# Cross-attention on one core: the first 512 keys of the probabilities stay unscaled, and their factors are applied when the values' product is copied out

## The chip, the cores and the metric

The kernel runs on one core of one Trainium2 chip. The metric is the device time of one execution in microseconds, the lower the better. Three runs of the kernel before took 2043.12, 2043.25 and 2043.85 us; the median is 2043.25 us. All data are float32. The core's engines are named as in the profile: PE (TensorE, the matmuls), PEld (its weight loads), DVE (VectorE), ACT (ScalarE), POOL (GpSimd) and SP (SyncE, which issues most DMAs).

## The reference, cut to what matters

Two cross-attention layers follow each other, over 8 batches with 100 queries, 20 heads of 32 columns, and a context of 722 tokens: 77 "text" tokens and 645 "ip" tokens. Each head has two softmaxes, one over the text keys and one over the ip keys, and their two products with the values are added:

```python
def attend(q, k, v):                       # one head: (S, 32), (L, 32), (L, 32)
    return softmax(q @ k.T / sqrt(32)) @ v
# layer 0
hs = attend(q, k_text, v_text) + attend(q, k_ip, v_ip)
x = hs @ Wo.T + bo + x
# layer 1: the ip scores get a term per (query, key), the ip probabilities a mask per query
hs = attend(q, k_text, v_text) + (softmax(q @ k_ip.T / sqrt(32) + 0.5 * sem) * mask[:, None]) @ v_ip
out = hs @ Wout + bout + x
```

Here q, k and v are projections of x and of the context; `sem` comes from a small attention of its own. The projections of the context (8 x 645 tokens x 1024, into 640 columns of keys and of values, for each of the two layers) are most of the arithmetic.

## The kernel before, in words

**Two streams of work.** The kernel forms the keys and values of a pair of batches ("production", tiles `psk_*`, `psv_*`, `psvk_*` with a Strassen-like scheme of seven products) and writes them to DRAM, and meanwhile it runs the attention of batches whose keys and values were made earlier. The order of PE, DVE and ACT is written out by hand (`manual_schedule` with the list `PINNED`, line 44): the loop at the end of the kernel goes through `ORDER`, 80 *steps* `(u, c)`, where `u` is one of 16 (layer, batch) units and `c` one of 5 groups of four heads. Between the pieces of a step it places production tasks by a plan of times (`production`, `between`). POOL and SP keep the order in which the instructions are recorded, or what the scheduler makes of it; POOL has little besides the DMAs that write the products to DRAM (lines 652, 691, 694, 811, 814, 841, 914).

**One step.** Steps are counted here from 0 to 79. In step n, with `last` for step n-1, the recorded order is: `scores(n, 0)` against the first 512 keys; production; `transposes(last, 0)` and `(last, 1)`; production; `transposes(last, 2)` and `(last, 3)`; `scores(n, 1)` against the other 210 keys (133 ip, 77 text); production; `transposes(last, 4)` and `(last, 5)`; production; `values(last)`. From step 74 on (`few`) the third stretch of production comes behind `transposes(last, 5)`. Where this text says t0 to t5 it means these six groups of four transposes (line 1099), one per block of 128 keys.

**The softmax of a step** (`scores`). The four heads' scores fall in two PSUM tiles. DVE takes the maxima (line 1003 in layer 0; line 1009 in layer 1, where it also adds `sem` and writes the sum to `p`). ACT takes the exponentials (line 1017) into the tile `p` of 100 queries x 4 heads x 722 keys, with the row sums. The two ranges of the ip keys have maxima of their own, so each has a correction factor `f`. `factors` (lines 1039 to 1043, DVE) combines the sums into `mul`, two factors per query and head (first 512 keys; the other 133), and `rz`, the text's reciprocal sum. Then `p` is scaled in place: ACT multiplies the first 512 keys of each head (`scaled`, line 1049, four instructions a step), DVE the 133 (line 1057) and the 77 (line 1053).

**Who runs what, when.** Exponentials, factors and scalings are not recorded in place but put on the list `later`, and `emit` hands them out between production tasks. `transposes(u, c, 0)` begins with `emit(len(later))`: whatever of the running step is then on the list (the exponentials of its first 512 keys) goes into ACT's queue ahead of the copies of t0.

**Transposes and values.** PE transposes `p` block by block into PSUM, 4 heads x 100 queries wide; the 400 columns are copied to the tile `pt`, by DVE for t0, t1, t3, t5 (line 1106) and by ACT for t2 and t4 (line 1104; in the transposes after the last step t0 too). `values` multiplies `pt` with the values (line 1122, 24 matmuls of 100 columns, four heads side by side in 32 columns of the array each) and DVE copies the 128 x 100 result into `hs` (line 1126), from which `out_piece` (line 904) makes the layer's output; for the last pair `last_out` does it (line 956, `pso_last`), in pieces between the last steps and behind them.

**Buffers.** `ps_pt` has two PSUM buffers, taken in turn by t0 to t5, by `values`, and by the small products (`pso`, `psq`, `psm`); so t2 must wait until t0 is copied out, and t3 until t1 is. `hs` has one buffer in the pool `one`, for a group of two units; a new group's first write must wait until `out_piece` has read the old one. `stats` holds maxima, sums and factors of a step.

Of the kernel before, what the change touches and what calls it, by code (L numbers as in the profile page):

```python
# [9 lines left out]
F32 = mybir.dt.float32  # L10
AF = mybir.ActivationFunctionType
ALU = mybir.AluOpType
AX = mybir.AxisListType

P = 128
B = 8
S = 100
# [3 lines left out]
NI = 645  # L21
NL = NI - 5 * P
NK = NI + NT
KA = 512
KB = NK - KA
H = 20
D = C // H
NC_ = C // P
# [10 lines left out]
PAIRS = [(2 * i, 2 * i + 1) for i in range(NU // 2)]  # L39

ORDER = [(u, c) for u in range(NU - 2) for c in range(NC_)]
# [5 lines left out]
def two_layer_xattn(  # L47
# [17 lines left out]
    nc = tc.nc  # L65
# [21 lines left out]
    ident = const.tile([P, P], F32, tag="ident", name="ident")  # L87
# [17 lines left out]
    wide = {}  # L105
# [152 lines left out]
    with ExitStack() as es:  # L258
# [6 lines left out]
        for k in range(NC_):  # L265
            t = fp.tile([P, C], F32, tag="wr", name=f"wq0_{k}", bufs=NCC)
            rows = wq[0][k * P : (k + 1) * P, :]
# [26 lines left out]
        ps = product_ps("zeros_ps")  # L294
# [4 lines left out]
        for g in range(B // 2):  # L299
            t = fp.tile([P, 2, NC_, S], F32, tag="q", name=f"q0_{g}", bufs=2)  # L300
            ps = [product_ps(f"psq_{g}_{i}") for i in range(3)]
            for k in range(NC_):
                for c in range(NC_):
                    at = c % 2 * 2 * S
                    nc.tensor.matmul(  # L305
                        ps[c // 2][:, at : at + 2 * S], lhsT=wq0[k][:, c * P : (c + 1) * P],
                        rhs=xt[:, 2 * g : 2 * g + 2, k, :],
                        start=(k == 0 and c % 2 == 0), stop=(k == NC_ - 1), skip_group_check=True,
# [174 lines left out]
    stat = ctx.enter_context(tc.tile_pool(name="stat", bufs=3))  # L483
# [483 lines left out]
            nc.sync.dma_start(out[LAST[i] % B][:, c0:c1], resg[g][:, i, c0:c1])  # L967


    pr, stats, sct = {}, {}, {}  # L970

    later = []

# [8 lines left out]
    def scores(u, c, part):  # L982
        k0, k1 = ((0, KA), (KA, NK))[part]
        if part == 0:
            pr[u, c] = ppool.tile([S, 4, NK], F32, tag="p", name=f"p_{u}_{c}")

            stats[u, c] = stat.tile([S, 14, 4], F32, tag="st", name=f"st_{u}_{c}")
        else:
            free_scores()

        scs = [ps_sc.tile([P, 2, 512], F32, tag=f"sc{h}", name=f"sc_{u}_{c}_{part}_{h}") for h in range(2)]
        for i in range(4):
            rows = slice(32 * i, 32 * i + 32)
            nc.tensor.matmul(  # L994
                scs[i // 2][:S, i % 2, : k1 - k0], lhsT=qs_[u][rows, c, :], rhs=ks[u, c][rows, k0:k1], start=True, stop=True
            )
        p, st, l = pr[u, c], stats[u, c], u // B
        n = min(k1, NI) - k0
        lo, f, rz, mul = st[:, 6, :], st[:, 7:9, :], st[:, 9:11, :], st[:, 11:13, :]

        def maxima(h):
            if l == 0:
                nc.vector.tensor_reduce(  # L1003
                    st[:, part, 2 * h : 2 * h + 2], scs[h][:S, :, :n], AX.X, ALU.max, negate=True
                )
                return
            for i in (2 * h, 2 * h + 1):

                nc.vector.tensor_tensor_reduce(  # L1009
                    out=p[:, i, k0 : k0 + n], in0=scs[h][:S, i % 2, :n], in1=sems[u][:, k0 : k0 + n], scale=-1.0,  # L1010
                    scalar=3.0e38, op0=ALU.add, op1=ALU.min, accum_out=st[:, part, i : i + 1],
                )

        def exponentials(h):
            for i in (2 * h, 2 * h + 1):
                dst = p[:, i, k0 : k0 + n]
                nc.scalar.activation(  # L1017
                    dst, dst if l else scs[h][:S, i % 2, :n], AF.Exp, bias=st[:, part, i : i + 1],
                    scale=-1.0 if l else 1.0, accum_out=st[:, 3 + part, i : i + 1],
                )  # L1020

        def text_maxima(h):
            heads = slice(2 * h, 2 * h + 2)
            nc.vector.tensor_reduce(st[:, 2, heads], scs[h][:S, :, n:KB], AX.X, ALU.max, negate=True)
            nc.vector.tensor_tensor(
                p[:, heads, NI:], scs[h][:S, :, n:KB], st[:, 2, heads].unsqueeze(2).to_broadcast([S, 2, NT]), ALU.add
            )

        def differences():

            nc.vector.tensor_tensor(lo, st[:, 0, :], st[:, 1, :], ALU.min)
            nc.vector.tensor_tensor(f, lo.unsqueeze(1).to_broadcast([S, 2, 4]), st[:, 0:2, :], ALU.subtract)

        def text_exponentials():
            nc.scalar.activation(f, f, AF.Exp)
            nc.scalar.activation(p[:, :, NI:], p[:, :, NI:], AF.Exp)

        def factors():
            nc.vector.tensor_reduce(st[:, 5, :], p[:, :, NI:], AX.X, ALU.add)
            nc.vector.tensor_tensor(st[:, 3:5, :], st[:, 3:5, :], f, ALU.mult)  # L1040
            nc.vector.tensor_tensor(st[:, 4, :], st[:, 3, :], st[:, 4, :], ALU.add)
            nc.vector.reciprocal(rz, st[:, 4:6, :])
            nc.vector.scalar_tensor_tensor(  # L1043
                mul, f, mask_sb[:, l : l + 1], rz[:, 0:1, :].to_broadcast([S, 2, 4]), ALU.mult, ALU.mult
            )

        def scaled(heads):
            for i in heads:
                nc.scalar.activation(p[:, i, :KA], p[:, i, :KA], AF.Copy, scale=mul[:, 0, i : i + 1])  # L1049

        def scaled_rest(text):
            if text:
                nc.vector.tensor_tensor(
                    p[:, :, NI:], p[:, :, NI:], rz[:, 1, :].unsqueeze(2).to_broadcast([S, 4, NT]), ALU.mult
                )
            else:
                nc.vector.tensor_tensor(
                    p[:, :, KA:NI], p[:, :, KA:NI], mul[:, 1, :].unsqueeze(2).to_broadcast([S, 4, NI - KA]),
                    ALU.mult,
                )  # L1060

        for h in range(2):
            maxima(h)
        if part == 0:
            later.append((True, lambda: exponentials(0)))
            later.append((True, lambda: exponentials(1)))
        else:
            for h in range(2):
                text_maxima(h)
            differences()  # L1070
            later.append((True, lambda: (exponentials(0), exponentials(1), text_exponentials())))
            if (u, c) == ORDER[-1]:

                later.append((False, factors))
                later.append((False, lambda: (
                    scaled((0, 1)),
                    nc.vector.tensor_tensor(
                        p[:, 2:, :KA], p[:, 2:, :KA], mul[:, 0, 2:].unsqueeze(2).to_broadcast([S, 2, KA]), ALU.mult
                    ),
                    scaled_rest(False), scaled_rest(True),  # L1080
                )))
                return
            later.append((False, lambda: (factors(), scaled_rest(False))))
            later.append((False, lambda: (scaled((0, 1)), scaled_rest(True))))
            later.append((False, lambda: scaled((2, 3))))

    pts = {}

    def transposes(u, c, j, at_end=False):
        if j == 0:  # L1090
            emit(len(later))
            pts[u, c] = one.tile([P, 6, 4 * S], F32, tag="pt", name=f"pt_{u}_{c}")
        rows = P if j < 5 else NTAIL
        if at_end and j in (2, 3):
            ps = ps_sc.tile([P, 2, 512], F32, tag=f"sc{j - 2}", name=f"pspt_{u}_{c}_{j}")[:, 0]
        else:
            ps = ps_pt.tile([P, 512], F32, tag="pt", name=f"pspt_{u}_{c}_{j}")
        for i in range(4):
            nc.tensor.transpose(  # L1099
                ps[:rows, i * S : (i + 1) * S], pr[u, c][:, i, j * P : j * P + rows], ident[:S, :S]  # L1100
            )
        dst, src = pts[u, c][:rows, j, :], ps[:rows, : 4 * S]
        if j in (2, 4) or at_end and j == 0:
            nc.scalar.copy(dst, src)  # L1104
        else:
            nc.vector.tensor_copy(dst, src)  # L1106

    def values(u, c):
        g, at = group_of[u]
        if g not in hsg:  # L1110

            hsg[g] = one.tile([P, 2, NC_, S], F32, tag="hs" if g < len(PAIRS) - 1 else "qst", name=f"hs_{g}")
        pt = pts[u, c]
        ps = ps_pt.tile([P, 512], F32, tag="pt", name=f"pv_{u}_{c}")
        for j in range(6):
            for i in range(4):
                if j < 5:
                    lhs = vs[u, c][:, j, i * D : (i + 1) * D]
                else:
                    lhs = vts[u][:, (4 * c + i) * D : (4 * c + i + 1) * D]  # L1120
                rows = P if j < 5 else NTAIL
                nc.tensor.matmul(  # L1122
                    ps[32 * i : 32 * i + 32, :S], lhsT=lhs, rhs=pt[:rows, j, i * S : (i + 1) * S],
                    start=(j == 0), stop=(j == 5),
                )
        nc.vector.tensor_copy(hsg[g][:, at, c, :], ps[:, :S])


    AHEAD = 1.2
# [299 lines left out]
```

## Time and profile before

| what | value |
|---|---|
| median of three runs | 2043.25 us (2043.12 to 2043.85) |
| span of the profiled execution | 2041.3 us |
| PE busy | 2024.2 us, 99% of the span |
| DVE, ACT, POOL busy | 1129.4, 783.1 and 274.2 us |
| granted TensorE clock | 1.000 |
| DMA | 252.20 MB, mean 124 GB/s |

The page gives the profiled execution's span, from the first to the last instruction, and no total beside it; the median of the runs is 1.95 us above the span. The table of busy times counts an engine as busy while at least one of its instructions is in flight. Matmuls are pipelined: the mean duration of one is longer than the distance from one to the next, so a price of a matmul is read from the distances in the timeline and not from the mean. In the list of waits a line reads: who waited, for whom, the sum in us, how often, the longest. In the timeline a line reads: start, length, engine, source line, operation, what is written from what, shapes, count, and in brackets the idle time before it and what ended it.

### The profile page before, as it was taken

To read this page: it belongs to the slowest core of one execution; us is meant where nothing else is said; L and a number is where in the kernel's file an instruction comes from. 1 tells how busy PE (TensorE), PEld (TensorE's weight loads), DVE (VectorE), ACT (ScalarE), POOL (GpSimd) and SP (SyncE) were. 2 spreads that over 40 slices of the span, in tenths; PEclk is the share of its full clock that TensorE was granted. 3 is DMA by queue.
4 is the path that set the end of the run, shared out by engine and by line. 5 is a ranking of instruction groups with operands and counts; after the bars stand their busy time and mean duration, and the time that the engine had idled before them with its cause. 6 is when DMAs were issued, how large, how long until landed. Compare 5 with 4: busy or idle time off the path is not lost.

```text
span 2041.3 us, 38689 instructions
## 1 busy us (share of the span) xinstructions
PE 2024.2 (99%) x15162; PEld 1568.8 (77%) x15162; DVE 1129.4 (55%) x3048; ACT 783.1 (38%) x2245; POOL 274.2 (13%) x433
## 2 busy tenths in 40 slices
PE   9999999999999999999999999999999999999998
PEld 9676768776876867778678777777777778889877
DVE  2223322245555465554657665655665667778787
ACT  1001000033433343333434444444544455566676
POOL 0001212111111101111111001001010101111110
PEclk9999999999999999999999999999999999999999
DMA  9544323323432533325256354236342536545461
GB/s 341 154 131 147 108 75 93 99 66 93 117 99 71 157 102 108 89 83 156 90 131 172 92 164 121 82 100 183 99 118 81 148 95 174 147 138 152 124 189 55
DMA packets 296628, 252.20 MB, mean 124 GB/s; under 512 B 46654, under 2 KB 265586, under 8 KB 296446
## 3 DMA queue, kind: packets, MB, share of 16 engines
q1 hardware_dynamic: 274398, 181.19, 32.8%
q0 software_dynamic: 21776, 68.44, 9.3%
q8 instruction: 119, 1.95, 0.4%
q14 instruction: 63, 0.52, 0.1%
q10 hardware_dynamic: 272, 0.10, 0.0%
HBM read 180.74 MB, written 68.93 MB: 122 GB/s over the span
## 4 chain that ended last, share of the span: by engine, by line
PE 95%; DVE 4%; ACT 1%; issue 0%; DMA 0%; SPq 0%; DVEq 0%
PE psv_a L637 9%; PE psv_d L637 8%; PE pspt L1099 8%; PE psk_a L667 8%; PE psk_d L667 7%; PE sc L994 6%; PE psv_e L637 4%; PE pv L1122 4%; PE psk_b L667 4%; PE psk_c L667 4%; PE psv_b L637 4%; PE psv_c L637 4%; PE psk_e L667 4%; PE pso L904 3%; PE psq L923 2%; PE psq L305 2%
## 5 line engine op out<-in xcount | busy, mean ns | idle before, releaser
L1017 ACT ACTIVATE p<-sc,st 100x512 f32<-100x512 f32 (+1 forms) x320 | 165.8, 530 | 201.8 <-DVE st L1003 120.0
L1049 ACT ACTIVATE p<-p,st 100x512 f32<-100x512 f32 x318 | 206.7, 713 | 46.2 <-DVE st L1043 45.9
L1099 PEld LDWEIGHTS pspt<-ident,p 100*128 100x128 f32 (+1 forms) x1920 | 187.1, 137 | 42.7 <-issue 5.3
L1106 DVE COPY pt<-pspt 128x400 f32<-128x400 f32 (+1 forms) x319 | 175.2, 568 | 77.8 <-PE pspt L1099 69.4
L1099 PE MATMUL pspt<-ident,p 100*128 100x100 f32 (+1 forms) x1920 | 209.6, 250 | 6.5 <-DVE pt L1106 2.1
L1017 ACT ACTIVATE p<-p,st 100x512 f32<-100x512 f32 (+1 forms) x320 | 176.6, 554 | 76.8 <-DVE st L1009 76.8
L637 PE MATMUL psv_a<-wv,x 128*128 128x397 f32 (+1 forms) x560 | 185.9, 474 | 0.6 <-DVE ko L228 0.3
L1104 ACT COPY pt<-pspt 128x400 f32<-128x400 f32 x161 | 79.1, 491 | 249.3 <-PE pspt L1099 248.9
L637 PE MATMUL psv_d<-wv,s 128*128 128x320 f32 (+1 forms) x560 | 174.4, 454 | 0.0
L691 POOL DMA_DIRECT2D k_d<-ko x140 | 100.0, 718 | 453.2 <-DVE ko L228 399.8
L637 PEld LDWEIGHTS psv_a<-wv,x 128*128 128x128 f32 x560 | 102.8, 189 | 68.4 <-issue 13.6
L1009 DVE CUSTOM_DVE_ANT_0 p<-sc,sem 100x512 f32<-100x512 f32 (+1 forms) x320 | 138.7, 490 | 21.9 <-PE sc L994 21.0
L637 PEld LDWEIGHTS psv_d<-wv,s 128*128 128x128 f32 x560 | 103.5, 190 | 52.6 <-issue 3.3
L1003 DVE TENSOR_REDUCE st<-sc 100x2 f32<-100x1024 f32 (+1 forms) x160 | 125.2, 824 | 28.8 <-PE sc L994 28.7
L994 PE MATMUL sc<-k,q 32*100 32x210 f32 (+1 forms) x1280 | 138.5, 502 | 0.0
L667 PE MATMUL psk_d<-s,wk 128*128 128x256 f32 (+1 forms) x672 | 136.7, 348 | 0.1
L667 PE MATMUL psk_a<-x,wk 128*128 128x256 f32 (+1 forms) x672 | 135.2, 346 | 0.0
L667 PEld LDWEIGHTS psk_d<-s,wk 128*128 128x128 f32 x672 | 108.5, 189 | 20.7 <-issue 6.7
L667 PEld LDWEIGHTS psk_a<-x,wk 128*128 128x128 f32 x672 | 109.5, 189 | 17.7 <-issue 4.5
L652 POOL DMA_DIRECT2D v_d<-vo x70 | 38.8, 554 | 624.6 <-DVE gst L627 318.7
L637 PE MATMUL psv_e<-wvt,x 128*128 128x397 f32 (+1 forms) x280 | 92.9, 474 | 0.0
L1122 PEld LDWEIGHTS pv<-pt,v 128*32 128x32 f32 x3200 | 67.5, 110 | 26.2 <-issue 17.2
(218 smaller groups left out, 3301.2 us busy)
## 6 DMA issues: line engine op xcount, KB each, us to landing
x<-ip_t SPq DMA_DIRECT2D x80, 512.0 KB
k<-k_d SPq DMA_DIRECT2D x80, 322.5 KB
v<-v_d SPq DMA_DIRECT2D x80, 320.0 KB
v_d<-vo POOLq DMA_DIRECT2D x70, 320.0 KB, 2.4
k_d<-ko POOLq DMA_DIRECT2D x112, 128.0 KB, 4.4
o<-wo SPq DMA_DIRECT2D x35, 320.0 KB
x<-ip_t SPq DMA_DIRECT2D x20, 532.0 KB
q<-wq SPq DMA_DIRECT2D x20, 320.0 KB
```

Of the source, the lines that this page charges most:

```text
L637: nc.tensor.matmul(ps[:, :m], lhsT=tokens(k)[:, :P], rhs=w[:, k, :], start=(k == 0 and not go_on), stop=(k == HK - 1), skip_group_check=True,)
L667: nc.tensor.matmul(ps[:, i * m : (i + 1) * m], lhsT=w[:, k, :], rhs=tokens(k), start=(i == 0 and k == 0 and not go_on), stop=(k == HK - 1) ...
L691: nc.gpsimd.dma_start(dst[:, :, r], src)
L994: nc.tensor.matmul(scs[i // 2][:S, i % 2, : k1 - k0], lhsT=qs_[u][rows, c, :], rhs=ks[u, c][rows, k0:k1], start=True, stop=True)
L1003: nc.vector.tensor_reduce(st[:, part, 2 * h : 2 * h + 2], scs[h][:S, :, :n], AX.X, ALU.max, negate=True)
L1009: nc.vector.tensor_tensor_reduce(out=p[:, i, k0 : k0 + n], in0=scs[h][:S, i % 2, :n], in1=sems[u][:, k0 : k0 + n], scale=-1.0, scalar=3.0e ...
L1017: nc.scalar.activation(dst, dst if l else scs[h][:S, i % 2, :n], AF.Exp, bias=st[:, part, i : i + 1], scale=-1.0 if l else 1.0, accum_out= ...
L1049: nc.scalar.activation(p[:, i, :KA], p[:, i, :KA], AF.Copy, scale=mul[:, 0, i : i + 1])
L1099: nc.tensor.transpose(ps[:rows, i * S : (i + 1) * S], pr[u, c][:, i, j * P : j * P + rows], ident[:S, :S])
L1104: nc.scalar.copy(dst, src)
L1106: nc.vector.tensor_copy(dst, src)
L1122: nc.tensor.matmul(ps[32 * i : 32 * i + 32, :S], lhsT=lhs, rhs=pt[:rows, j, i * S : (i + 1) * S], start=(j == 0), stop=(j == 5),)
```

## The change

Four things change together.

- `scaled` is gone: the first 512 keys of `p` stay as the exponentials left them. The 133 keys are scaled by ACT, one instruction for each head, in place of one DVE instruction for the four (in the last step it stays with DVE). The 77 text keys are scaled by DVE as before.
- `values` writes into two ranges of 100 columns of its PSUM tile: the products of key blocks 0 to 3 (the 512 unscaled keys) into the first, those of blocks 4 and 5 into the second.
- The first range is multiplied by its factor when it is copied out, and the second is added: two DVE instructions in place of the copy. Since the product has head columns on the partitions and queries on the columns, the factors are needed in that layout: POOL spreads `mul[:, 0, :]` (100 x 4) over 32 columns a head into the new tile `wide` (100 x 128, one buffer), PE transposes it behind t5 into the columns 400 to 500 of t5's PSUM tile, and ACT copies these to the place in `hs` where the result will stand.
- Copies change hands: t0 and t5 are copied by ACT now, so ACT has t0, t2, t4 and t5 and DVE t1 and t3. The buffer of `hs` is taken at t5 and not at `values`.

```diff
@@ scores @@
-            stats[u, c] = stat.tile([S, 14, 4], F32, tag="st", name=f"st_{u}_{c}")
+            stats[u, c] = stat.tile([S, 11, 4], F32, tag="st", name=f"st_{u}_{c}")
...
-        lo, f, rz, mul = st[:, 6, :], st[:, 7:9, :], st[:, 9:11, :], st[:, 11:13, :]
+        lo, f, rz, mul = st[:, 6, :], st[:, 7:9, :], st[:, 4:6, :], st[:, 9:11, :]
...
-        def scaled(heads):
-            for i in heads:
-                nc.scalar.activation(p[:, i, :KA], p[:, i, :KA], AF.Copy, scale=mul[:, 0, i : i + 1])
+        def widened():
+            wide[u, c] = one.tile([S, P], F32, tag="wide", name=f"wide_{u}_{c}")
+            nc.gpsimd.tensor_copy(
+                wide[u, c].rearrange("p (i d) -> p i d", i=4), mul[:, 0, :].unsqueeze(2).to_broadcast([S, 4, D])
+            )
...
+            elif (u, c) != ORDER[-1]:
+                for i in range(4):
+                    nc.scalar.activation(p[:, i, KA:NI], p[:, i, KA:NI], AF.Copy, scale=mul[:, 1, i : i + 1])
...
-                later.append((False, lambda: (
-                    scaled((0, 1)),
-                    nc.vector.tensor_tensor(
-                        p[:, 2:, :KA], p[:, 2:, :KA], mul[:, 0, 2:].unsqueeze(2).to_broadcast([S, 2, KA]), ALU.mult
-                    ),
-                    scaled_rest(False), scaled_rest(True),
-                )))
+                later.append((False, lambda: (widened(), scaled_rest(False), scaled_rest(True))))
                 return
-            later.append((False, lambda: (factors(), scaled_rest(False))))
-            later.append((False, lambda: (scaled((0, 1)), scaled_rest(True))))
-            later.append((False, lambda: scaled((2, 3))))
+            later.append((False, factors))
+            later.append((False, lambda: (widened(), scaled_rest(False), scaled_rest(True))))
+
+    def heads_sum(u, c):
+        g, at = group_of[u]
+        if g not in hsg:
+            hsg[g] = one.tile([P, 2, NC_, S], F32, tag="hs" if g < len(PAIRS) - 1 else "qst", name=f"hs_{g}")
+        return hsg[g][:, at, c, :]
@@ transposes @@
-        if j in (2, 4) or at_end and j == 0:
+        if j == 5:
+            nc.tensor.transpose(ps[:, 4 * S : 5 * S], wide[u, c], ident[:S, :S])
+            nc.scalar.copy(heads_sum(u, c), ps[:, 4 * S : 5 * S])
+        if j in (0, 2, 4, 5):
             nc.scalar.copy(dst, src)
         else:
             nc.vector.tensor_copy(dst, src)
@@ values @@
                 nc.tensor.matmul(
-                    ps[32 * i : 32 * i + 32, :S], lhsT=lhs, rhs=pt[:rows, j, i * S : (i + 1) * S],
-                    start=(j == 0), stop=(j == 5),
-                )
-        nc.vector.tensor_copy(hsg[g][:, at, c, :], ps[:, :S])
+                    ps[32 * i : 32 * i + 32, j // 4 * S : (j // 4 + 1) * S], lhsT=lhs,
+                    rhs=pt[:rows, j, i * S : (i + 1) * S], start=(j in (0, 4)), stop=(j in (3, 5)),
+                )
+        hs = heads_sum(u, c)
+        nc.vector.tensor_tensor(hs, ps[:, :S], hs, ALU.mult)
+        nc.vector.tensor_tensor(hs, ps[:, S : 2 * S], hs, ALU.add)
```

More of the change, by code (lines that the diff above doesn't have):

```diff
@@ L967, in last_out_add @@
             nc.sync.dma_start(out[LAST[i] % B][:, c0:c1], resg[g][:, i, c0:c1])
-    pr, stats, sct = {}, {}, {}
+    pr, stats, sct, wide = {}, {}, {}, {}
     later = []
@@ L1108, in values @@
     def values(u, c):
-        g, at = group_of[u]
-        if g not in hsg:
-            hsg[g] = one.tile([P, 2, NC_, S], F32, tag="hs" if g < len(PAIRS) - 1 else "qst", name=f"hs_{g}")
         pt = pts[u, c]
```

## The prediction

> **What bounds the kernel.** I read the page's busy times, the slices with the granted clock, the windows, the list of what PE waited for, the timeline of a steady step, and last the timeline and the chain of waits of the final steps.
>
> From the page:
>
> ```profile
> PE 2024.2 (99%) x15162; PEld 1568.8 (77%) x15162; DVE 1129.4 (55%) x3048; ACT 783.1 (38%) x2245; POOL 274.2 (13%) x433
> ...
> PEclk9999999999999999999999999999999999999999
> ```
>
> From the windows (stretch, its length, then busy us of PE, PEld, DVE, ACT and POOL, clock, DMA share, GB/s):
>
> ```profile
> 433.00:1750.00 1317.00, 1315.67 (x9898) 1011.74 (x9900) 777.05 (x2054) 556.78 (x1605) 170.44 (x266) 1.00 0.41 117
> 1750.00:1950.00 200.00, 196.32 (x2216) 173.12 (x2205) 157.83 (x529) 119.79 (x346) 27.69 (x39) 1.00 0.51 140
> 1950.00:2041.00 91.00, 82.87 (x1050) 68.42 (x1048) 73.00 (x257) 62.76 (x178) 10.96 (x18) 0.99 0.41 117
> ```
>
> PE is the bound at full clock. In the 1317 us that hold steps 1 to 59 it idles 1.3 us; from 1750 on 3.7 and 8.1 us. All that a relief of other engines can win there lies in the last 290 us. The list of PE's waits says what these gaps are:
>
> ```profile
> PE pspt L1099 <- DVE pt L1106: 2.1, 8, 0.6
> PE pspt L1099 <- DVE res L909: 2.0, 9, 0.6
> ...
> PE pspt L1099 <- ACT p L1049: 0.5, 2, 0.3
> ```
>
> PE hardly ever waits for the scaling that is removed (line 1049: 0.5 us in two places). It waits for PSUM buffers of the transposes. The timeline of a steady step gives the distances:
>
> ```profile
> 548.27 0.85 PE L1099 MATMUL pspt<-ident,p 100*128 100x100 f32 x8
> 548.96 1.92 PE L667 MATMUL psk_c<-x,wkt 128*128 128x256 f32 x8
> ```
>
> Eight transposes take 0.69 us before the next group starts: 86 ns each, though the group's mean of one is 250 ns. The last steps run in another mode (step 78):
>
> ```profile
> 2009.78 0.71 DVE L1057 TENSOR_TENSOR p<-p,st 100x532 f32<-100x532 f32 x1
> 2009.84 2.56 ACT L1049 ACTIVATE p<-p,st 100x512 f32<-100x512 f32 x4 [1.12 <-DVE st L1043]
> ...
> 2010.80 0.25 DVE L1126 COPY hs<-pv 128x100 f32<-128x100 f32 x1
> 2010.97 0.68 DVE L1009 CUSTOM_DVE_ANT_0 p<-sc,sem 100x512 f32<-100x512 f32 x1
> ...
> 2012.31 0.71 ACT L1017 ACTIVATE p<-p,st 100x512 f32<-100x512 f32 x1
> ...
> 2013.41 1.05 DVE L1106 COPY pt<-pspt 128x400 f32<-128x400 f32 x2
> ...
> 2014.04 1.04 PE L1099 MATMUL pspt<-ident,p 100*128 100x100 f32 x8 [0.65 <-DVE pt L1106]
> ...
> 2014.42 0.71 ACT L1017 ACTIVATE p<-p,st 100x512 f32<-100x512 f32 x1
> ...
> 2015.13 0.47 ACT L1104 COPY pt<-pspt 128x400 f32<-128x400 f32 x1
> ```
>
> There is little production left to cover the softmax. DVE scales, adds up, takes four maxima, copies t0 and t1; PE stands until t0 is out (idle 0.65 us), then t2 and t3, second scores, t4, t5. ACT's four exponentials end only at 2015.11.
>
> **The change, part by part.**
>
> *PE: one transpose a step.* 80 more, of the same form as 1600 there (100x128 weights, 100 columns). From the distance, 80 x 0.086 = **6.9 us**; from the group's busy time, 181.3/1600 = 0.113, it is 9.0 us; the shortest distance I find, eight from 700.38 to 701.06, gives 6.8. I take 6.9: the new one stands behind four of its kind. PE has no idle time in steps 1 to 59 to hide it in. The 24 value matmuls keep number and shape, so the two ranges cost PE nothing; the added waits on ACT between them are met early except at the end, below.
>
> [...]
>
> *DVE* loses the 0.71 us of line 1057 (79 steps) and two copies of 0.57, and gains one instruction near 0.26 (line 1126's copy has the form): -1.6 us a step, 125 us in all. Off PE's path in steps 1 to 59: worth 0 there.
>
> *ACT* loses 4 x 0.64 (distance, 2.56 for four) = 2.56 a step. It gains four scalings of 133 keys: the exponentials of 133 and of 512 keys differ by 0.71 - 0.40 = 0.32, so 0.64 - 0.32 = 0.32 each, 1.3 for four; two copies of 0.49 and one of 100 columns between 0.23 (128x77, line 623) and 0.34 (128x200, line 927). Together about 0 a step. What counts is their place. In the changed program's order of instructions t0's copy stands behind the exponentials of the running step's first scores, and t5's ahead of the exponentials of its second scores from step 74 on.
>
> *POOL* gets one spreading a step. The row nearest to it is 128x308 in 0.84 us (line 128); by size 0.35. It stands among DMA issues of 0.54 to 0.72 us, at most eight in a row (5.8 us), and waits for DVE's factors and PE's transpose of the step before; the stores of keys and values queue behind it for as long. They are due a step (11 to 31 us) or more later, and t5 comes 6 us after the factors even in step 78 (2009.75 to 2016.0). I take 0; if that cover went, 79 steps each waited.
>
> *The buffer of hs* is now taken at t5. At seven changes of group ACT's copy of the factors must wait until `out_piece` of the old group has its last read, which stands behind t5 in PE's order with one product between (1.73 + 1.71 us). ACT is held for 3.4 us, and behind it t5's copy, the scalings and the next exponentials. Another product (1.73) precedes `values`, and ACT needs 0.7 of it: 0; without that cover 7 x 0.7 = 5 us. The smaller `stats` tile: 0.
>
> *Steps 60 to 77.* In step 64 the transposes wait 0.9 us in all for line 1049 (its scaling runs to 1819.2): -0.8. In step 72, t0 follows the scores after 1.05 us and t2 waits for t0's copy by DVE until 1944.1; by ACT it follows the exponentials, which end at 1944.7, so t2 moves from 1944.24 to 1945.3: +1.1. Steps 60, 62, 65, 66 and 71 have t2 5.4 us behind the scores, where ACT's exponentials end 4.6 to 5.1 behind them; with the copy 0 to 0.25 late each: +0.5. Steps 73 to 77: t2 comes 0.26 later, but t3, which waited for DVE's second copy, then follows at once: 0.
>
> *Steps 78, 79 and the end.* Two ACT copies (0.39 and 0.2 of distance) now stand ahead of the second exponentials: factors +0.6. DVE then saves line 1057 (-0.64) and adds the second hs instruction, which waits for the first (+0.3): maxima +0.25. The scaling is shorter, so exponentials start with the first maximum and end near 2014.8; t0's copy ends 2015.3 and t2 starts there and not at 2014.04: +1.3, of which t3's lost wait returns 0.3. Second scores +1.0, and the exponentials behind t5's copy +1.5. Step 79 repeats it from there: +2.4 at its factors. Line 956 then waits for the second hs instruction (+0.3); behind it five ACT copies in a row take what the dropped scaling of 512 keys leaves. End: **+2.7**. Bounds: if only DVE's shortening counts, 0.64 + 0.57 - 0.3 = 0.9 a step wins 1.8; if both steps pay t0's copy and t5's in full and again behind the last step, +5.
>
> Sum: 6.9 - 0.8 + 1.1 + 0.5 + 2.7 = 10.4 us. 2041.3 + 10.4 = 2051.7, and with the 1.95 us around the span 2053.6. I say **2053.5 us**, 0.5% slower.
>
> **Rivals.**
>
> *The relief pays the end.* Shorter DVE chains win 1.8 us there, step 72 costs nothing, and step 64's 0.8 comes back: 6.9 - 2.6 = +4.3, 2047.5. For it: DVE is 73 of 91 us busy at the end. Against it: ACT is 62.8 of 91 and gets the copies in its worst place.
>
> *Faster.* PE's stalls behind the softmax go, all of them: 3.7 + 8.1 = 11.8 us of idle from 1750 on, less 6.9: -4.9, 2038.4. It decides from 11 us won. Against it: 2.8 us or more of this idle is for `res`, `sem`, `tp` and the tail, which the change doesn't touch.
>
> *The factors come late from POOL.* Each t5 waits 0.2 us behind a row of DMA issues: 79 x 0.2 = 16 more, 2069. For it: POOL's idle is spent waiting for products, so its issues bunch. Against it: the 6 us above.
>
> *The hs buffer holds ACT* long enough for PE at the seven changes: +5, 2058.5.
>
> **How the numbers follow.** Main case 0.64; relief 0.14; faster 0.06; POOL 0.07; hs buffer 0.09. A measurement of this kernel tells about 0.2%, 4.1 us, from no change: 2039.2 to 2047.3. The relief case straddles the upper bound: half of it is same. Faster 0.06, same 0.09, slower 0.85. Range: low end the relief case at 2047.0, high end the main case with transposes at 9.0 and the end at +5 (+4.4), and the hs buffer's 2058.5: 2059.
>
> **What would show it.** The same clock; 1920 + 80 transposes with a distance near 86 ns; DVE some 125 us less busy, ACT about as busy, and neither moving the steady steps, each 0.09 us longer. In the last steps t2 waiting for ACT's copy of t0, which starts as the fourth exponential ends, and periods over 11 us in place of 10.3. In step 64 no wait for scaled `p`. POOL's spreading ends before t5 everywhere. The prediction is wrong if PE's list of waits gains a line for POOL or for ACT's copies in the steady steps, or if the last steps get shorter.

## The result

The changed kernel takes 2055.77 us in the median of five executions (2052.77 to 2055.83) against 2043.12 us for five of the kernel before: ratio 1.0058, 95% interval 1.0046 to 1.0071. It is slower, near the forecast of 2053.5 us and inside its range. The profiled execution is the quickest of the five, 2052.77 us with a span of 2051.0 us, so it shows 9.7 us of the surplus; the other four are 2.5 to 3.1 us longer, and where those lie is found further down.

From the page of the changed kernel:

```profile
PE 2030.5 (99%) x15242; PEld 1576.8 (77%) x15242; DVE 1025.7 (50%) x2889; ACT 761.2 (37%) x2482; POOL 301.4 (15%) x513
...
PEclk9999999999999999999999999999999999999999
```

DVE lost 104 us and ACT 22 us of busy time, and the kernel is slower: PE is 99% busy, at full clock. (Added up instruction by instruction, DVE lost 122 us and ACT 3, near the 125 and the 0 of the forecast; the busy time counts stretches in which two instructions overlap once.) The windows of the changed kernel (columns as before) show where PE still idles:

```profile
433.00:1750.00 1317.00, 1314.74 (x9890) 1011.97 (x9889) 698.39 (x1928) 537.38 (x1773) 187.13 (x320) 1.00 0.40 116
1750.00:1950.00 200.00, 196.84 (x2234) 174.28 (x2232) 139.80 (x491) 116.49 (x379) 34.05 (x54) 1.00 0.49 138
1950.00:2051.00 101.00, 88.88 (x1109) 74.05 (x1107) 66.67 (x264) 64.88 (x216) 14.47 (x27) 0.99 0.41 118
```

DVE is 79 us less busy in the first stretch, and by this view PE gains nothing there: its idle time went from 1.3 to 2.3 us. In the last stretch it went from 8.1 to 12.1 us. What PE waited for, from the list of waits after:

```profile
PE pspt L1103 <- ACT pt L1111: 3.7, 4, 1.7
PE pso_last L956 <- DVE hs L1131: 1.8, 2, 1.1
...
PE pv L1125 <- DVE res L909: 1.6, 3, 0.5
```

The transposes now wait 3.7 us for ACT's copies, in four places; `pso_last` waits 1.8 us for the second `hs` instruction (0.8 before); and the value product has a wait of its own in three places. No line names POOL. The timeline of a steady step shows the transpose that was added:

```profile
557.57 0.85 PE L1103 MATMUL pspt<-ident,p 100*128 100x100 f32 x8
558.26 0.25 PE L1108 MATMUL pspt<-ident,wide 100*128 100x100 f32 x1
558.34 2.86 PE L637 MATMUL psv_a<-wv,x 128*128 128x397 f32 x8
```

It has a duration of 0.25 us and takes PE 0.08 us, from 558.26 to 558.34. The rest of the reading goes by the lengths of the 80 steps, from the start of one step's first scores on PE to the next. In us against the kernel before (step 79 goes to the end of the span; steps 0 and 56 are within 0.02):

| step | 16 | 26 | 36 | 31, 41 | 55 | 61 | 64 | 70 | 72 | 73 | 78 | 79 | 45, 52, 59, 67, 74 | most others |
|---|---|---|---|---|---|---|---|---|---|---|---|---|---|---|
| changed | -0.58 | -0.30 | -0.30 | +0.68 each | +0.56 | +0.29 | -0.63 | -0.53 | +0.74 | +0.45 | +0.90 | +1.92 | +0.13 to +0.19 | +0.05 to +0.10 |

A step's length repeats between kernels wherever nothing near it was changed (in the last experiment below, 73 of the steps 0 to 78 are within 0.03 us of the kernel before), so single terms can be read from one profile, far below what the times of whole executions tell apart.

The largest wait is the one in step 78. The timeline of the changed kernel there, PE, ACT and DVE:

```profile
2018.56 0.72 ACT L1017 ACTIVATE p<-p,st 100x512 f32<-100x512 f32 x1
...
2019.38 0.85 PE L1103 MATMUL pspt<-ident,p 100*128 100x100 f32 x8
...
2020.28 0.57 DVE L1113 COPY pt<-pspt 128x400 f32<-128x400 f32 x1
...
2020.69 0.71 ACT L1017 ACTIVATE p<-p,st 100x512 f32<-100x512 f32 x1
...
2021.40 0.47 ACT L1111 COPY pt<-pspt 128x400 f32<-128x400 f32 x1
...
2021.93 0.91 PE L1103 MATMUL pspt<-ident,p 100*128 100x100 f32 x8 [1.70 <-ACT pt L1111]
```

PE has t0 and t1 in PSUM at 2020.2. DVE copies t1 out at once, but t0's copy stands on ACT behind the fourth exponential and starts at 2021.40. PE stands for 1.70 us, where it stood 0.65 us before.

### The profile page after: what moved, and what is told of

Read it like the earlier page. It is cut to its first block, busy times and chain, and to the rows that moved or that the text cites. A ratio compares the mean times of both kernels' runs of the same rounds, so it can differ in the third digit from the quotient of the medians.

```text
span 2051.0 us, 39249 instructions
## 1 busy us (share of the span) xinstructions
PE 2030.5 (99%) x15242; PEld 1576.8 (77%) x15242; DVE 1025.7 (50%) x2889; ACT 761.2 (37%) x2482; POOL 301.4 (15%) x513
## 4 chain that ended last, share of the span: by engine, by line
PE 96%; DVE 2%; ACT 2%; issue 0%; DVEq 0%; ACTq 0%
PE psv_a L637 9%; PE psv_d L637 8%; PE psk_d L667 8%; PE pspt L1103 8%; PE psk_a L667 8%; PE sc L994 6%; PE pv L1125 4%; PE psv_e L637 4%; PE psk_c L667 4%; PE psk_b L667 4%; PE psk_e L667 4%; PE psv_b L637 4%; PE psv_c L637 4%; PE pso L904 3%; PE psq L305 2%; PE psq L923 2%
## 5 line engine op out<-in xcount | busy, mean ns | idle before, releaser
L1111 ACT COPY pt<-pspt 128x400 f32<-128x400 f32 x320 | 157.1, 491 | 285.7 <-PE pspt L1103 285.2
L1113 DVE COPY pt<-pspt 128x400 f32<-128x400 f32 x160 | 91.8, 574 | 81.9 <-PE pspt L1103 79.2
L1060 ACT ACTIVATE p<-p,st 100x133 f32<-100x133 f32 x316 | 102.2, 398 | 24.7 <-DVE st L1043 24.2
```

The source lines that it names most:

```text
L1060: nc.scalar.activation(p[:, i, KA:NI], p[:, i, KA:NI], AF.Copy, scale=mul[:, 1, i : i + 1])
```

## Experiments

**One transpose more, nothing else.** The kernel before, with

```diff
+        if j == 5:
+            nc.tensor.transpose(ps[:, 4 * S : 5 * S], pr[u, c][:, 3, 4 * P : 5 * P], ident[:S, :S])
```

> The kernel before with one transpose more behind t5 in each step, into the free columns 400 to 500 of t5's PSUM tile; it reads a block of p that is there already, and nothing reads it. Theory (PE is the bound, a transpose costs its distance): 80 x 0.086 = +6.9 us, 2050.0 us, 1.0034 of before, and the steps longer by 0.09 each. Rival A (the changed kernel's time comes from ACT and POOL, the transposes lie beside other work): within 1 us of before. Rival B (a transpose costs PE the 0.25 us of its mean): +20 us, 2063.

Measured: 2049.88 us (2048.26 to 2050.66) beside 2043.64 us for the kernel before on the same chip, ratio 1.0030 (1.0019 to 1.0042). The steps from 1 on are 0.05 to 0.10 us longer, but 16, 26, 36, 56, 61, 64, 70 and 78 only 0.00 to 0.02: there PE waits for another engine, and the transpose lies in the wait. From step 0 to the end that makes 6.1 us. The theory holds, rivals A and B fall. The one transpose a step has a duration of 0.25 us here too and takes PE 0.08 us (557.45 to 557.53); 80 durations would have made the 20 us of rival B.

**The changed kernel without its transpose.**

```diff
-            nc.tensor.transpose(ps[:, 4 * S : 5 * S], wide[u, c], ident[:S, :S])
-            nc.scalar.copy(heads_sum(u, c), ps[:, 4 * S : 5 * S])
+            nc.scalar.copy(heads_sum(u, c), ident[:, :S])
```

> The changed kernel without the transpose of the factors: ACT copies 100 columns of the identity matrix from SBUF into hs in its place, so the factors are not applied (the output is not the reference's); POOL's spreading and all copies and their places stay. Theory: -6.9 us against the changed kernel, which is 2046 to 2049, and the last steps as long as in the changed kernel. Rival A (ACT and POOL cost the time): within 1 us of the changed kernel. Rival B (0.25 us a transpose): -20 us.

Measured: 2049.35 us (2047.98 to 2050.97), ratio 1.0029 (1.0018 to 1.0040), 6.4 us below the changed kernel. The seven executions lie on two levels, three at 2048.0 to 2048.7 and four at 2049.4 to 2051.0, and the profile is of one of the four. In the profiles steps 0 to 77 take 1604.47 us and not 1610.75: 6.3 us less, with the steady steps as long as before the change (within 0.03 us). POOL's spreading, ACT's scalings and all copies are still there, so they cost the steady steps nothing. But step 78 was 14.75 us long, 3.1 us longer than in the changed kernel. The windows of this kernel say why (columns as above, the clock third from the end):

```profile
2012.00:2014.00 2.00, 1.79 (x18) 1.60 (x17) 2.00 (x9) 1.89 (x6) 0.00 (x0) 1.00 0.33 87
2014.00:2016.00 2.00, 0.43 (x3) 0.43 (x4) 0.49 (x2) 1.51 (x5) 0.00 (x0) 0.88 0.26 77
2016.00:2022.00 6.00, 6.00 (x35) 5.22 (x35) 2.86 (x15) 3.46 (x14) 0.00 (x0) 0.50 0.00 0
2022.00:2024.00 2.00, 2.00 (x50) 1.90 (x52) 1.52 (x6) 0.63 (x3) 0.40 (x1) 0.91 0.00 0
```

PE stood 1.77 us for t0's copy, and from 2015.5 to 2022.35 its granted clock was 0.50. This gave the idea for the fifth experiment.

**Copies of t0 and t5 back to DVE.**

```diff
-        if j in (0, 2, 4, 5):
+        if j in (2, 4) or at_end and j == 0:
```

> The changed kernel with the copies of t0 and t5 given back to DVE (behind the last step ACT keeps t0, as before). Theory (the place of ACT's two copies costs the end 2.7 us, and step 72 another 0.7): -3 us against the changed kernel, 2050 to 2053; step 78 is 10.8 us long and not 11.6, t2 of step 78 starts 4.9 us behind its first scores and not 5.9, step 72 is 11.5 long and not 12.2; steady steps unchanged. Rival (the end is longer by the factors' way, transpose, copy and second DVE instruction, and not by the copies' place): within 0.5 us of the changed kernel, steps 78 and 79 as long as there.

Measured: 2051.08 us (2050.59 to 2051.41), ratio 1.0038 (1.0024 to 1.0053), 4.7 us below the changed kernel's median and 2.2 us below its quickest execution (lowest to lowest). Against the kernel before, step 72 is +0.19, step 78 -0.33, from step 79 to the end +0.68. The place of the copies therefore cost 0.90 + 0.33 + 1.92 - 0.68 = 2.5 us at the end and 0.55 in step 72; the rival, for which these steps should have stayed, falls. Steps 31, 41 and 61 got worse (+1.10, +1.10, +0.84): with t5's copy on DVE the waits at a change of group are longer.

**Factors in a tile of their own.** They are copied back into `wide` (made 128 x 128), and `hs` is taken at the multiplication:

```diff
-            nc.scalar.copy(heads_sum(u, c), ps[:, 4 * S : 5 * S])
+            nc.scalar.copy(wide[u, c][:, :S], ps[:, 4 * S : 5 * S])
...
-        nc.vector.tensor_tensor(hs, ps[:, :S], hs, ALU.mult)
+        nc.vector.tensor_tensor(hs, ps[:, :S], wide[u, c][:, :S], ALU.mult)
```

> The changed kernel with the transposed factors copied into their own tile (wide, once it has been transposed) and not into hs, so that hs is taken at the multiplication, as before, and not at t5. Theory: only the seven changes of group move; steps 31 and 41, each 0.68 us longer in the changed kernel than before, lose that again: -1.4 us against the changed kernel. Rival (the hand-off of hs costs nothing, and the two steps are longer by chance of the order): 0 us, and steps 31 and 41 stay at 26.9 us.

Measured: 2053.40 us (2050.52 to 2053.57), ratio 1.0046 (1.0031 to 1.0061), 2.4 us below the changed kernel. Steps 31 and 41 are +0.09 and step 61 -0.30: 0.59 less in each of the three, 1.8 us; the other 0.8 us is won in steps 45 to 72, most of it in step 55 (+0.18 in place of +0.56). The theory holds, and it missed the third change of group that it concerns. The timeline of the changed kernel in step 31 shows the hold:

```profile
1172.11 1.85 PE L904 MATMUL pso<-hs,o 128*128 128x200 f32 x10
1174.00 0.24 ACT L1109 COPY hs<-pspt 128x100 f32<-128x100 f32 x1 [3.75 <-PE pso L904]
...
1174.14 0.49 ACT L1111 COPY pt<-pspt 82x400 f32<-82x400 f32 x1
...
1174.48 1.07 PE L1125 MATMUL pv<-pt,v 128*32 128x100 f32 x40 [0.52 <-DVE res L909]
```

ACT stands 3.75 us with the factors' copy until `pso` has read the old `hs`; behind it comes t5's copy, and the value product, which is next on PE with no production between, waits. The trace puts that wait down to `res` on DVE (1174.01 to 1174.43). In the kernel with the own tile the product starts ahead of the end of `res`. There its first matmul waits for a semaphore of ACT, which had passed long before, and in the changed kernel for one of DVE. Read so, the two kernels give the product different buffers of `ps_pt`: t5's there, and here, where t5's is held until ACT's copy ends at 1174.63, the one of `pso`, which `res` frees. The hold reaches PE by way of the buffer.

In the profile with the own tile, too, PE stood 1.69 us in step 78 and the clock fell. Its windows:

```profile
2018.00:2020.00 2.00, 0.31 (x4) 0.30 (x4) 0.63 (x3) 1.65 (x5) 0.00 (x0) 0.99 0.43 125
2020.00:2026.00 6.00, 6.00 (x37) 5.22 (x35) 2.86 (x15) 3.20 (x14) 0.00 (x0) 0.50 0.00 0
2026.00:2028.00 2.00, 2.00 (x38) 1.90 (x41) 1.43 (x6) 0.63 (x3) 0.00 (x0) 0.80 0.00 0
```

From 2019.98 to 2026.8 the clock is 0.50. Steps 78 and 79 together are 2.9 us longer than in the changed kernel's profile. Three of this kernel's four executions lie at 2053.2 to 2053.6 and one at 2050.5: the same 3 us as between the changed kernel's executions.

**The gap filled.** In step 78 alone:

```diff
+        if j == 1 and (u, c) == ORDER[77]:
+            for _ in range(12):
+                nc.tensor.transpose(ps[:, 4 * S : 5 * S], pr[u, c][:, 3, P : 2 * P], ident[:S, :S])
```

> The changed kernel with twelve transposes more in step 78 alone, between t1 and t2, into free columns, read by nothing: they fill some 1.0 us of the 1.70 us for which PE stands there until ACT has copied t0. Theory of the clock (where PE does nothing for 1.5 us or more, its clock can be halved for the next 6.8 us, which costs 3 us, and this is what parts the changed kernel's executions at 2055.3 to 2055.8 from the one at 2052.8): no wait over 1.1 us is left ahead of step 79, the clock stays 1.00 to the end in every execution, all of them take 2052.5 to 2053.3, and step 78 is 11.6 to 11.7 us long. Rival (the 3 us have another cause, such as a DMA or the order on an engine): executions at both 2052.8 and 2055.6, as in the changed kernel.

Measured: 2052.75 us (2052.55 to 2053.57, five executions), ratio 1.0048 (1.0035 to 1.0060); twelve transposes more and 3 us quicker than the changed kernel's median. Its timeline, with the same start of t2 as in the changed kernel:

```profile
2019.37 0.85 PE L1103 MATMUL pspt<-ident,p 100*128 100x100 f32 x8
2020.06 1.19 PE L1112 MATMUL pspt<-ident,p 100*128 100x100 f32 x12
...
2021.91 0.91 PE L1103 MATMUL pspt<-ident,p 100*128 100x100 f32 x8 [0.66 <-ACT pt L1114]
```

Every execution is at the lower level, and step 78 is 11.61 us long, as in the changed kernel's profile. The mean granted clock of an execution says the same: 0.998 in the changed kernel's four longer executions and 0.999 in its quickest, 0.999 to 1.000 in all five here; 6.8 us at half clock take 0.0017 off the mean. The clock theory holds for these executions. Its 1.5 us was the author's estimate, from the falls behind the waits of 1.77 and 1.69 us above; no run shows a limit there (with t5's copy alone on DVE, below, a fall came behind 1.30 us).

**t0's copy alone back to DVE.**

```diff
-        if j in (0, 2, 4, 5):
+        if j in (2, 4, 5) or at_end and j == 0:
```

> The changed kernel with t0's copy alone given back to DVE. Theory (each of the two copies costs the end at its own place: t0's holds t2, t5's holds the running step's second exponentials): step 78 is 10.6 to 10.8 us long (11.61 in the changed kernel, 10.71 before), t2 4.9 us behind the first scores; step 79 to the end keeps about half of its surplus, 22.6 us (23.37 and 21.41). End -1.6 us against the changed kernel, step 72 back to 11.5 to 11.6 from 12.17; 2050.5 to 2051, without the 3 us of the halved clock, since the 1.7 us wait is gone. Rival (only both copies together hold anything, ACT's queue being full either way): steps 78 and 79 within 0.3 us of the changed kernel's.

Measured: 2050.07 us (2049.90 to 2050.67), ratio 1.0035 (1.0021 to 1.0048). Step 72 is 11.63 us, step 78 is 10.72 us with t2 at 4.88 us, from step 79 to the end 22.56 us: all as the theory has it. PE's wait for t2 is the 0.67 us of before, and by its line it is DVE's copy again:

```profile
2019.93 1.04 PE L1103 MATMUL pspt<-ident,p 100*128 100x100 f32 x8 [0.67 <-DVE pt L1113]
```

The copy of t0 alone thus costs 0.89 + 0.80 us at the end, 0.54 in step 72 and 0.6 in steps 45, 52 and 55 (+0.09 each here), besides the halved clock. Most of the 0.6 goes with the own tile as well: in step 55 DVE's first maximum starts 1.64 us behind the scores in the changed kernel and 1.26 to 1.29 with either mending, and the copy of t0, which stands behind the exponentials, is later by as much. Why DVE starts late there was not traced.

**t5's copy alone back to DVE.**

```diff
-        if j in (0, 2, 4, 5):
+        if j in (0, 2, 4):
```

> The changed kernel with t5's copy alone given back to DVE. Theory: t2 of step 78 still waits for ACT's copy of t0 (1.5 us or more, and with it the halved clock in most executions); the second exponentials of steps 78 and 79 come 0.4 us earlier each, so the end wins 0.8 to 1.2 us: 2051.7 where the clock holds and 2054.7 where it doesn't. The three changes of group cost more than in the changed kernel (steps 31 and 41 +0.4 each, as when both copies were on DVE). Rival (t5's copy by ACT costs nothing, ACT catches up before the next wait): steps 78 and 79 within 0.2 us of the changed kernel's.

Measured: 2053.81 us (2053.55 to 2054.63), ratio 1.0052 (1.0037 to 1.0067). Of the theory, the end came out: second scores of step 78 start 6.34 us behind the first and not 6.74, step 79 to the end is 0.58 us shorter. The total did not: steps 31 and 41 lost 0.42 each, step 61 0.54, and step 64 another 0.8, where a product waits 0.79 us for ACT's copy. The wait in step 78 is 1.30 us here, and the profile has a halved clock of 3.4 us (2024.8 to 2028.2).

**The 133 keys on ACT, in the kernel before.**

```diff
+            elif (u, c) != ORDER[-1]:
+                for i in range(4):
+                    nc.scalar.activation(p[:, i, KA:NI], p[:, i, KA:NI], AF.Copy, scale=mul[:, 1, i : i + 1])
...
-            later.append((False, lambda: (factors(), scaled_rest(False))))
+            later.append((False, factors))
...
-            later.append((False, lambda: scaled((2, 3))))
+            later.append((False, lambda: (scaled((2, 3)), scaled_rest(False))))
```

> The kernel before with one part of the change alone: the 133 keys scaled by ACT, four instructions a step behind the scaling of the 512 keys, and not by DVE (the last step stays). No transpose is added, p is scaled as before. Theory (steps 16, 26, 36 and 70 of the changed kernel are 0.4 to 0.7 us shorter because DVE has line 1057 no more): these four shorten by 0.67, 0.38, 0.38 and 0.6, -2.0 us in all; the steady steps stay as they are though ACT gets 1.6 us more a step; step 64 and the last two lose 1 to 2 us, since the scaling of p ends 1.6 us later there. Sum -1 to +1 us. Rival (they are shorter because ACT has the 512 keys no more): the four stay as before, and the kernel is 1 to 2 us slower.

Measured: 2043.40 us (2043.23 to 2045.63), ratio 1.0004 (0.9995 to 1.0013), no difference. Steps 16, 26, 36 and 70 are -0.67, -0.38, -0.37 and -0.52, and step 61 -0.39: the relief is DVE's, and the rival, for which these steps should have stayed, falls. Step 63 loses 0.73 and step 64 wins 0.74. Steps 78 and 79 lose 1.17 each. Here t4 waits 1.53 us for ACT, and three of ten executions lie 2 us above the others; their mean clocks (0.998 and 0.999) do not part them from those (0.998 to 1.000), so the cause of these 2 us is open.

**Everything mended but the transposes.** Factors in their own tile, and

```diff
-        if j in (0, 2, 4, 5):
+        if j in (2, 4) or j in (0, 5) and ORDER.index((u, c)) < 70 or at_end and j == 0:
```

> The changed kernel with everything mended that the runs so far blame, the extra transposes left: the transposed factors in a tile of their own (as in own_factor_tile), and t0 and t5 of the products from index 70 on copied by DVE. Theory (the changed kernel's surplus is transposes, hold of hs, place of ACT's copies and halved clock, and they add up): steps 31 and 41 +0.09 against before, step 61 -0.3, step 72 +0.2, step 78 -0.3, step 79 +0.7; span 9.7 - 0.6 x 3 - 0.4 - 0.55 - 1.2 - 1.3 = +4.4 against before, 2045.7, time 2047.5, with no halved clock; still slower than before by 0.2%, since the transposes' 6.2 us exceed the 2.5 us that steps 16, 26, 36, 61, 64 and 70 win. Rival (the terms hang together, one mending takes what another gives): 2049 or more.

Measured: 2047.75 us (2047.27 to 2048.24, ten executions) beside 2043.16, ratio 1.0021 (1.0012 to 1.0030). Steps 31 and 41 are +0.09, 61 -0.30, 72 +0.09, 78 -0.33, 79 +0.88: the terms add up. From step 0 to the end it takes 4.25 us more than before, less than the 6.1 us that the transposes alone cost: what is left over of the change wins 1.85 us, and the transposes take more than it wins.

**The relief without the transposes.** As in the experiment with the 133 keys on ACT, but for the products of index 0 to 69 only:

```diff
+        early = ORDER.index((u, c)) < 70
...
-            elif (u, c) != ORDER[-1]:
+            elif early:
```

> The kernel before with the 133 keys scaled by ACT for the products of index 0 to 69 (behind the scaling of the 512 keys), by DVE from index 70 on, as before. Theory (relief of DVE alone makes steps 16, 26, 36, 61 and 70 shorter, and it needs no transpose): these five -0.67, -0.38, -0.37, -0.39 and -0.52, steps 63 and 64 +0.73 and -0.74, the last ten as before: -2.3 us, 2040.6 to 2041.2, ratio 0.9989, no halved clock. Rival (the gain of step 70 or of the others needs ACT late in the last steps too): -1 us or less.

Measured: 2041.39 us (2040.80 to 2042.37, eleven executions) beside 2043.16, ratio 0.9991 (0.9982 to 1.0000): 1.8 us quicker, with the interval's end at no difference. The steps came out as expected but for step 70, which stays as before: it is index 70's own scaling that has to leave DVE for it. A border at 71 was not run.

## Why the prediction came out, term by term

| term | predicted, us | measured, us | from |
|---|---|---|---|
| 80 transposes | +6.9 | +6.1 | before with the transpose alone, step 0 to the end |
| hold of `hs` at changes of group | 0 (bound 5) | +1.8 | steps 31, 41, 61, changed kernel less own tile |
| t0's copy late by a little in single steps | +0.5 | +0.6 | steps 45, 52, 55, changed kernel less t0 on DVE (most of it goes with the own tile too) |
| steps 59 and 67 | 0 | +0.2 | also gone with the own tile; not traced |
| step 64 | -0.8 | -0.65 | changed, less the transpose alone |
| step 72 | +1.1 | +0.64 | the same |
| steps 73, 74 | 0 | +0.44 | the same |
| steps 78, 79 and end | +2.7 | +2.7 | 0.90 + 1.92 - 0.08, the last being the transposes' part |
| DVE's relief in steps 1 to 63 and 70 | 0 | -2.1 | steps 16, 26, 36, 61, 70, against before with the transpose alone, without the hold in 61 |
| sum | +10.4 | +9.8 | from the start of step 0 on (the terms above make 9.7); it starts 0.14 us earlier, so the span is +9.7 |
| halved clock | none | +3 in four of five | gap filled: 2052.75 in place of 2055.77 |

*The main theory was right.* PE is the bound and a transpose costs it its distance. Most of the 0.8 us by which the term was too high are the eight steps in which PE waits anyway; the sentence that PE has no idle time in steps 1 to 59 to hide it in was wrong for 16, 26, 36 and 56.

*The end was right, place and size.* t2 waits for t0's copy (step 78: 5.91 us behind the first scores, 4.86 before), second scores follow 0.91 later, and t5's copy holds the next exponentials. The parts came out as 1.7 us for t0 and, with both on DVE against t0 alone, 0.34 + 0.45 = 0.8 for t5; the last 0.3 stays with both on DVE.

*Step 72 was right in the sum alone, and that was luck.* The text had t2 come 1.1 us later there, and nothing in steps 73 to 77. In the trace the first four of the later transposes start 4.34 us behind the scores (4.23 before), since they wait for DVE's copy of t1, and only the next four wait for ACT's copy of t0: 0.45 us, start at 5.36 in place of 4.71. So that t2 waits for t0 and t3 for t1 holds in step 78, but not here. The rest came in step 73: its value product waits 0.97 us for ACT's copy of t4, where before it waited 0.66 for DVE's copy of t5, and it does so with t5 back on DVE too.

*Costed at nothing, and not nothing: the hold of `hs`.* The step that failed is "another product precedes `values`, and ACT needs 0.7 of it: 0". In PE's order at the changes in steps 11, 21 and 51 a `psk` product stands between the last `pso` and `values`, as the text says; in steps 31, 41 and 61 `values` follows `pso` directly, so the cover isn't there, and in step 71 no `pso` is left to wait for. The mechanism (ACT held 3.4 us; 3.75 measured) was in the text, and its rival had 0.7 for each place (0.59 measured); what was missing was a look at each change of group by itself.

*Costed at nothing, and not nothing: DVE's relief.* "Off PE's path in steps 1 to 59: worth 0 there" was read from a total idle of 1.3 us. The step lengths show -0.67, -0.38 and -0.38 in steps 16, 26 and 36 (the 133 keys on ACT alone). The timeline of step 16 before shows where, PE and DVE:

```profile
802.60 0.71 DVE L1057 TENSOR_TENSOR p<-p,st 100x532 f32<-100x532 f32 x1
802.78 0.85 PE L1099 MATMUL pspt<-ident,p 100*128 100x100 f32 x8
803.23 0.42 DVE L222 TENSOR_TENSOR ko<-psk_d,ko 128x256 f32<-128x256 f32 x1
...
803.70 2.00 PE L667 MATMUL psk_d<-s,wk 128*128 128x256 f32 x8
```

The same with the 133 keys on ACT:

```profile
803.17 0.85 PE L1102 MATMUL pspt<-ident,p 100*128 100x100 f32 x8
803.86 1.92 PE L667 MATMUL psk_d<-s,wk 128*128 128x256 f32 x8
```

The production product `psk_d` waits until DVE has added the last one up (line 222), and that stands behind the scaling of line 1057. Without the scaling it follows the transposes after 0.69 us and not 0.92. The next product waits likewise for DVE's line 228, as it does in steps 26 and 36. In step 61 PE waits 0.57 us for `res`, in step 70 0.56 us for DVE's copy of t5. In step 16 the trace counts only 0.16 us before the two products as idle though 0.67 are lost, so the total idle was no bound for what a relief can win.

These two misses, +1.8 and -2.1, nearly cancelled, which is why the sum looked better than its parts.

*The text's own sign of being wrong came.* It was a new line for ACT's copies in PE's list of waits, in the steady steps. Of the four places of that line (3.7 us) three are in steps 72, 78 and 79, but one, 0.24 us, is in step 55; and the holds in steps 31 and 41 are in steady steps as well. That nothing but the transpose moves the steady steps was wrong.

*Not foreseen: the halved clock.* The forecast had "the same clock", and the profile of the changed kernel shows it, since it is of the one execution that kept it. The longer wait in step 78 (0.65 us before, 1.70 after) was priced by what it delays alone, t2 by 1.3 us (1.05 measured); in four executions of five another 3 us came with it (2055.77 us, and 2052.75 with the gap filled). The forecast of 2053.5 lies between the two levels, 0.75 us above the one at full clock (2052.75 with the gap filled) and 2.3 below the median.

*The late copies of t0* came in size by luck, since they came in steps 45, 52 and 55; in the five steps that the text named (60, 62, 65, 66, 71) there was nothing beyond the transpose.

*The rivals.* POOL never held t5. The rival "the relief pays the end" had the relief in the wrong place: it came, 2.1 us, but in steps 16, 26, 36, 61 and 70, and paid for the hold.

## What to carry to other kernels

Where one engine is 99% busy, a change that relieves the others and gives that engine one instruction a step more is priced by the distance of that instruction, times the steps (here 80 x 0.086 = 6.9 us, and 6.1 measured); the relief paid here only in steps where the bound engine waits (2.1 us in five of 80), and these are found by comparing step lengths between two traces, not from shares of busy time. A copy that frees a PSUM buffer belongs on the engine whose queue is short at that moment, which at the end of a kernel can be another one than in its middle (here t0's copy on ACT cost 1.7 us at the end, and t5's on DVE 0.42 us more in each of steps 31 and 41). Before a buffer is taken earlier, every place where it changes hands has to be looked at by itself (the hold of `hs` cost 0.59 us in each of three of the seven).

## What the runs showed that was not expected

**In three profiles the granted clock was 0.50 for 3.4 or 6.8 us behind a PE wait of 1.3 to 1.8 us.** At the end of a wait of 1.77 us (without the factors' transpose) and 0.3 us behind one of 1.69 us (own factor tile) the granted clock fell to 0.50 for 6.8 us, and 2.0 us behind one of 1.30 us (t5's copy on DVE) for 3.4 us. The step with the first of these was 14.75 us long, against 11.61 in the changed kernel. It does not come each time: the changed kernel's profiled execution has the wait of 1.70 us with the clock at 1.00, and so has that with the 133 keys on ACT alone, with its wait of 1.53 us. The changed kernel's four longer executions have no profile. That the clock was halved in them is inferred from the times, from their lower mean clock (0.998), from the two profiles with the waits of 1.77 and 1.69 us, and from the run in which twelve transposes shortened the wait to 0.66 us and all five executions were at the lower level. In the profiles of the kernel before and of the changed kernel the clock is 1.00 in every microsecond up to PE's last product, also behind waits of 1.39 us (both) and 1.27 us (changed, step 79). How long a wait has to be, and why 1.69 us went ahead of a fall in one execution and 1.70 us did not in another, is open.
